# Graph attention on gathered rows: a third result buffer, 25 row buffers for 26, and another assignment of buffers and places to the row gathers

## The chip, the core and the metric

One core of one Trainium2 chip. The core has five engines with a queue each: TensorE (PE, with its weight loads shown as PEld), VectorE (DVE), ScalarE (ACT), GpSimd (POOL) and SyncE (SP). Each engine executes its own instructions strictly in the order in which they stand in its queue, and an instruction waits on semaphores for what other engines or transfers must have finished. The metric is device time of one execution in microseconds (us). Eleven runs of the kernel before gave a median of 1240.71 us, from 1235.78 to 1246.11.

## What is computed

```python
def _L0_gnn_ref(x, adj, Wf, bf, Wg, bg, W, bW):
    f = x @ Wf + bf
    g = x @ Wg + bg
    e = jax.nn.relu(f @ g.T)
    scores = jnp.where(adj > 0, e, -9e15)
    attention = jax.nn.softmax(scores, axis=1)
    return attention @ (x @ W + bW)

h = jnp.maximum(_layernorm(x, axis=-1), 0.0)
x = x + _L0_gnn_ref(h, adj, Wf, bf, Wg, bg, W, bW)
```

There are 3327 nodes with 1024 features in fp32. The adjacency has ones on its diagonal, is symmetric, and has few neighbours in a row (one entry in 208 or so), so that scores are needed only between a node and its neighbours.

## The kernel before

**Part 1 (to about 245 us)** reads the adjacency, sorts each row's neighbours into a list, normalises x into `hd` in DRAM, forms the product matrix `A_sb` of Wf and Wg on TensorE, and sorts the nodes by their number of neighbours, so that tiles of 128 nodes have like numbers. The change doesn't touch this part.

**Part 2 (from about 245 us)** handles 26 tiles of 128 nodes, t = 0 to 25, in the order of the list `ORDER`. `CAPS` says how many neighbours a tile's nodes have at most: 37 in the largest tile, which is t = 2, down to 11. The steps of a tile are named by letters in the kernel's own plan, and this text uses the same names:

- `L` (POOL): an indirect DMA brings the tile's lists of neighbours (128 short rows) into SBUF. `M` (DVE, L1197) makes a mask from them. `C` and `F` do the like for the few lists longer than 24.
- `H` (POOL): an indirect DMA gathers the tile's own 128 rows of `hd` (512 KB) into a row buffer. `hT`, `q` (PE) and `hc`, `qc`, `fq` (ACT) turn and multiply them to the query q of the tile.
- `G(t,k)` (POOL, L635): an indirect DMA gathers, for each of the 128 nodes, the row of its k-th neighbour (512 KB) into a row buffer.
- `d(t,k)` (DVE, L1222): the dot product of such a row with q, which gives a score. It is the first reader of the row.
- `S`, `T` (DVE) and `E`, `A`, `Y` (ACT): softmax of the scores, in one or two chunks of k.
- `s(t,k)` (DVE, L1272) adds row k, times its weight, to the tile's sum; or else `w(t,k)` (ACT, L1256) scales it and `p(t,k)` (PE, L1260) adds it in PSUM while it transposes. `SHARE` fixes which k go which way. The last of these readers frees the row buffer.
- `yt`, `W` (PE), `yc`, `fo` (ACT): the sum is turned and multiplied by W. `rc(t,o)` (ACT, L1298) copies the two halves of the result into a result buffer.
- `X(t)` (POOL): an indirect DMA adds the tile's rows of x to the result buffer; `O(t)` (POOL, L1305) then scatters the buffer to the output. The buffer is free when O has landed.

**The row buffers** (`G`, ROWS of them, 512 KB each) hold H rows and G rows. **The result buffers** (`xp`) are two; tile t uses buffer t mod 2, so `rc(t)` waits until `O(t-2)` has landed.

**The order** of all steps on PE, DVE, ACT and POOL is computed when the kernel is built, by a planner in the kernel's text. `steps_of` lists 2544 steps on these engines and on the DMA, each with the engine, how long it holds the engine, how long until its result can be used, and what it depends on. A gather is entered as 1.31 us on POOL and 3.2 us on the DMA, a list as 1.31 and 2.2 us, an output scatter as 1.31 and 3.2 us. `forward` simulates the engines with these figures, `backward` gives every step a rank, `planned` repeats both 30 times with small random changes of the ranks (fixed seed) and keeps the plan that ends first. The result is a list of (due time, step, row buffer). The kernel then emits the steps in the order of the due times. On the chip a due time is not a timer: what is left of the plan is the order on each engine and which buffer a row gets. A gather is issued when POOL reaches it and the last reader of its buffer has finished. In the plan before, a row takes the buffer that has been free for longest.

Of the kernel before, what the change touches and what calls it, by code (L numbers as in the profile page):

```python
# [13 lines left out]
ALU = mybir.AluOpType  # L14
# [22 lines left out]
QS = 2  # L37
WS = 2
TURNS = 6.0
ROWS = 26  # L40
PASSES = 30
SEED = 1
WIDE = 0.6
# [285 lines left out]
def steps_of():  # L329

    steps = {}

    def add(engine, takes, lasts, name, *deps, **kw):
        steps[name] = Step(name, engine, takes, lasts, deps, **kw)

    chunks = [split(s) for s in ORDER]
    n = len(ORDER)
    add("DVE", 0.15, 0.2, ("fl", 0), at=265.0)
    for t, s in enumerate(ORDER):
        cap, ends = CAPS[s], chunks[t]  # L340
        add("POOL", 1.31, 1.31, ("L", t), ("M", t - 3), *(("G", t - 3, k) for k in range(CAPS[ORDER[t - 3]] if t > 2 else 0)))
        add("DMA", 0.4, 2.2, ("Ld", t), ("L", t))
        if t > 1:
            add("POOL", 1.31, 1.31, ("H", t), row=True)
            add("DMA", 1.33, 3.2, ("Hd", t), ("H", t))
            for g in range(2):
                add("PE", 0.44, 0.66, ("hT", t, g), ("Hd", t), ("hc", t - 1, g), ("hT", t, g - 1), frees=[("H", t)] * g)
            for g in range(2):
                add("ACT", 0.49, 0.6, ("hc", t, g), ("hT", t, g), *(("q", t - 1, i, j) for i in range(3) for j in range(QS)))
            for i in range(3):  # L350
                for j in range(QS):
                    add(
                        "PE", 4.66 / QS, 4.66 / QS + 0.2, ("q", t, i, j), ("hc", t, 0), ("hc", t, 1), ("fq", 3 * t + i),
                        ("q", t, i, j - 1),
                    )
                add(
                    "ACT", 0.4, 0.52, ("qc", t, i), ("q", t, i, QS - 1),
                    *(("d", t - 2, k) for k in range(CAPS[ORDER[t - 2]])),
                )
                if 3 * t + i + 2 < 3 * n:  # L360
                    add("ACT", 0.38, 0.48, ("fq", 3 * t + i + 2), ("qc", t, i))
        used = [(op, t - 3, k) for op in "swY" for k in range(KM)]
        add("DVE", 0.16, 0.25, ("M", t), ("Ld", t), ("S", t - 3, 0), ("S", t - 3, 1), ("rc", t - 3, 0), ("rc", t - 3, 1), *used)
        if s < MORE:
            add("POOL", 1.31, 1.31, ("C", t), ("F", t - 1))
            add("DMA", 0.4, 2.5, ("Cd", t), ("C", t))
            add("DVE", 1.3, 1.4, ("F", t), ("Cd", t), *(("G", t - 1, k) for k in range(KL, CAPS[ORDER[t - 1]])))
        if t == n - 1:
            add("POOL", 1.31, 1.31, ("x", t), row=True)
            add("DMA", 1.33, 3.2, ("xd", t), ("x", t))  # L370
        summed = []
        for c, (k0, k1) in enumerate(ends):
            last = c == len(ends) - 1
            for k in range(k0, k1):
                late = [("F", t)] if k >= KL else [("hc", 2, 1) if k < 6 else ("qc", 2, 1)] if t == 1 else []
                add("POOL", 1.31, 1.31, ("G", t, k), ("Ld", t), *late, row=True)
                add("DMA", 1.33, 3.2, ("Gd", t, k), ("G", t, k))
                add(
                    "DVE", 1.2, 1.38, ("d", t, k), ("Gd", t, k), *(("qc", t, i) for i in range(3)),
                    ("M", t), at=(256.0, 266.0)[t] if t < 2 else 0.0,  # L380
                )
            add("DVE", 0.48 if c else 0.29, 0.6 if c else 0.41, ("S", t, c), *(("d", t, k) for k in range(k0, k1)), ("M", t))
            if c:
                add("ACT", 0.28, 0.33, ("A", t), ("S", t, c))
            add("ACT", 0.48, 0.55, ("E", t, c), ("S", t, c), ("fl", t))
            if c:
                add("ACT", 1.05, 1.15, ("Y", t, c), ("A", t), *(("s", t, k) for k in range(1, k0)))
            else:
                add("ACT", 1.05, 1.15, ("Y", t, c), ("E", t, c))
            add("DVE", 0.25 * c + 0.11 * last + 0.01, 0.25 + 0.2 * c, ("T", t, c), ("E", t, c), *([("A", t)] if c else []))  # L390
            for k in range(max(k0, 1), k1):
                if k in on_tensor(t):
                    add("ACT", 1.05, 1.15, ("w", t, k), ("E", t, c))
                    add("PE", 0.873, 1.07, ("p", t, k), ("w", t, k), ("yc", t - 1, 0), ("yc", t - 1, 1), frees=[("G", t, k)])
                    summed.append(("p", t, k))
                else:
                    add("DVE", 1.2, 1.28, ("s", t, k), ("E", t, c), ("Y", t, c), frees=[("G", t, k)])
                    summed.append(("s", t, k))
        for o in range(2):
            add("ACT", 0.62, 0.72, ("fo", t, o), ("rc", t - 1, o), ("T", t, len(ends) - 1))  # L400
        for g in range(2):
            add(
                "PE", 0.44, 0.66, ("yt", t, g), *summed, ("Y", t, len(ends) - 1), ("yc", t - 1, 0), ("yc", t - 1, 1),
                ("yt", t, g - 1),
                frees=[("G", t, 0)] * g,
            )
        for g in range(2):
            add("ACT", 0.49, 0.6, ("yc", t, g), ("yt", t, g), *(("W", t - 1, o, j) for o in range(2) for j in range(WS)))
        for o in range(2):
            for j in range(WS):  # L410
                add(
                    "PE", 7.0 / WS, 7.0 / WS + 0.2, ("W", t, o, j), ("yc", t, 0), ("yc", t, 1), ("fo", t, o),
                    ("W", t, o, j - 1),
                )
            if t < n - 1:
                add("ACT", 0.62, 0.72, ("rc", t, o), ("W", t, o, WS - 1), ("Od", t - 2))
            else:
                add("DVE", 0.6, 0.7, ("rc", t, o), ("W", t, o, WS - 1), ("Od", t - 2), ("xd", t), ("rc", t, o - 1), frees=[("x", t)] * o)
        if t < n - 1:
            add("POOL", 2.05, 2.05, ("X", t), ("rc", t, 0), ("rc", t, 1))  # L420
            add("DMA", 2.0, 4.5, ("Xd", t), ("X", t))
        add("POOL", 1.31, 1.31, ("O", t), ("Xd", t), ("rc", t, 0), ("rc", t, 1))
        add("DMA", 1.33, 3.2, ("Od", t), ("O", t))
    for step in steps.values():
        step.deps = [steps[d] for d in step.deps if d in steps]
        for d in step.deps:
            d.after.append(step)
    return list(steps.values())
# [121 lines left out]
def planned(rows, passes, seed=0, wide=1.0):  # L550
# [11 lines left out]
    for _ in range(passes):  # L562
# [7 lines left out]
        for k in steps:  # L570
            k.rank += chance.gauss(0, wide)
    return best


@with_exitstack
def edge_path(ctx: ExitStack, tc: tile.TileContext, x, adj, Wf, bf, Wg, bg, W, bW, out, flag):
# [57 lines left out]
    def gather(to, table, idx, **kw):  # L634
        return nc.gpsimd.indirect_dma_start(  # L635
            out=to,
            out_offset=None,
            in_=table,
            in_offset=bass.IndirectOffsetOnAxis(ap=idx, axis=0),
            **kw,  # L640
        )
# [484 lines left out]
    def tiles(name, n, shape, dtype=FP, **kw):  # L1126
        pool = ctx.enter_context(tc.tile_pool(name=name, bufs=n, reuse_waits="tile", **kw))
        return [pool.tile(shape, dtype, name=name) for _ in range(n)]

    with tc.manual_schedule(engines={  # L1130
# [6 lines left out]
        more = tiles("more", 1, [P, KM - KL], I32)[0]  # L1137
        hT = tiles("hT", 1, [P, KD, P])[0]
        yT = tiles("yT", 1, [P, KD, P])[0]
        res = tiles("xp", 2, [P, O])  # L1140
        junk = tiles("junk", 1, [P, D], BF)[0]
        scs = tiles("sc", 3, [P, KM])
        masks = tiles("mask", 3, [P, KM])
        nms, ls = tiles("nm", 6, [P, 1]), tiles("l", 6, [P, 1])
        als, rss = tiles("al", 3, [P, 1]), tiles("rs", 3, [P, 1])
        one, worst, onesf = tiles("one", 3, [P, 1])
        ps_q = tiles("p_q", 2, [P, CB], space=PSUM)
        ps_t = tiles("p_t", 2, [P, 4, P], space=PSUM)
        ps_y = tiles("p_y", 2, [P, 4, P], space=PSUM)
# [140 lines left out]
                )  # L1290

        def rc(t, o):
            to = res[t % 2][:, o * CB : (o + 1) * CB]
            if t == NT - 1:
                xr = G[buf["x", t]][:, o * CB : (o + 1) * CB]
                nc.vector.scalar_tensor_tensor(to, ps_o[o], rss[t % 3], xr, op0=ALU.mult, op1=ALU.add)  # L1296
            else:
                nc.scalar.activation(to, ps_o[o], AF.Copy, scale=rss[t % 3])  # L1298

        def X(t):  # L1300
            gather(res[t % 2], x[:, :], perm[:, ORDER[t] : ORDER[t] + 1], compute_op=ALU.add)

        def scatter(t):
            whole = ORDER[t] < N // P
# [2 lines left out]
                out_offset=bass.IndirectOffsetOnAxis(  # L1307
                    ap=perm[:, ORDER[t] : ORDER[t] + 1] if whole else final, axis=0
                ),
                in_=res[t % 2],  # L1310
                in_offset=None,
                bounds_check=None if whole else N - 1,
                oob_is_err=whole,
# [9 lines left out]
            "fq": fq, "d": dot, "S": greatest, "A": A, "E": E, "Y": Y, "T": T, "w": w, "p": p, "s": s, "fo": fo, "yt": yt,  # L1323
            "yc": yc, "W": project, "rc": rc, "X": X, "O": scatter,
        }
        plan = sorted(planned(ROWS, PASSES, SEED, WIDE)[1], key=lambda step: step[0])
        for start, (op, *at), held in plan:
            if held is not None:
                buf[(op, *at)] = held
            made[op](*at)  # L1330
# [41 lines left out]
```

## Time and profile before

| what | us |
|---|---|
| median of 11 runs | 1240.71 |
| the profiled execution | 1238.72 |
| its span (first to last instruction) | 1236.9 |
| DVE busy | 1131.5 |
| PE busy | 1111.9 |
| POOL busy | 874.0 |
| ACT busy | 617.3 |
| part 1, up to the last preparation on DVE | 243.3 |
| 454 G gathers: POOL time of one | 1.15 |
| 468 d: DVE time of one | 1.285 |
| 257 s: DVE time of one | 1.286 |

The mean granted clock of TensorE was 0.958 of full speed. DMA queue q0 carries what POOL issues and moved 290.96 MB of 374.46 MB. Busy shares say how full an engine is; what the end is made of shows where an engine that is full has to wait.

### The profile page before, as it was taken

What the parts mean: (1) busy time and instruction counts of PE and PEld (TensorE: products, weight loads), DVE (VectorE), ACT (ScalarE), POOL (GpSimd) and SP (SyncE); (2) the same over time, 40 slices, a digit from 0 to 9 for tenths busy, and PEclk for the clock granted to TensorE, in tenths of its full rate; (3) what the DMA queues carried; (4) which work ended last, traced back from release to release, by engine and by line L of the source; (5) the groups of instructions that cost most, each with busy time, mean ns of one, the idle gap of its engine ahead of it and who ended that gap; (6) DMA issues with size and microseconds to landing.
All of it is one profiled execution on the core that took longest, in us unless ns stands there. A gap on an engine that the chain in (4) does not pass through costs nothing. (4 is left out here: it accounts for less than half of the span.)

```text
span 1236.9 us, 14478 instructions
## 1 busy us (share of the span) xinstructions
PE 1111.9 (90%) x4632; PEld 711.1 (57%) x4632; DVE 1131.5 (91%) x2167; ACT 617.3 (50%) x941; POOL 874.0 (71%) x677
## 2 busy tenths in 40 slices
PE   2799981698889899998999999999998999999995
PEld 1566650466647466666765666665655665655552
DVE  5899987867999999999999999999999999999990
ACT  6899979225617266435644355444433333333260
POOL 8999986177577776777776777557667776777721
PEclk8799996799889999999999999999999999999998
DMA  9999996679858998989998998879988998899841
GB/s 367 418 402 404 410 350 249 243 275 370 301 208 291 350 304 318 332 315 306 337 331 286 321 323 313 274 216 349 322 291 263 324 279 300 273 321 300 297 123 53
DMA packets 101803, 374.46 MB, mean 303 GB/s; under 512 B 14747, under 2 KB 18490, under 8 KB 98519
## 3 DMA queue, kind: packets, MB, share of 16 engines
q0 software_dynamic: 80624, 290.96, 68.9%
q1 hardware_dynamic: 21094, 82.49, 17.3%
q8 instruction: 38, 0.62, 0.2%
q14 instruction: 47, 0.39, 0.1%
HBM read 344.11 MB, written 29.30 MB: 302 GB/s over the span
## 5 line engine op out<-in xcount | busy, mean ns | idle before, releaser
L635 POOL DMA_INDIRECT G<-hd,ps x454 | 521.6, 1149 | 212.3 <-issue 82.9
L1222 DVE CUSTOM_DVE_ANT_0 junk<-G,q 128x1024 bf16<-128x1024 f32 x468 | 601.3, 1285 | 27.5 <-DMA G<-hd,ps 19.5
L1287 PE MATMUL p_o<-W_sb,yT 128*128 128x512 f32 x832 | 366.2, 595 | 0.7 <-ACT yT L1283 0.7
L1209 PE MATMUL p_q<-A_sb,hT 128*128 128x342 f32 x1152 | 353.4, 456 | 6.8 <-ACT p_q L1218 6.1
L1272 DVE SCALAR_TENSOR_TENSOR G<-G,sc 128x1024 f32<-128x1024 f32 x257 | 330.4, 1286 | 3.0 <-ACT G L1245 1.9
L1209 PEld LDWEIGHTS p_q<-A_sb,hT 128*128 128x128 f32 x1152 | 213.8, 191 | 112.0 <-issue 9.7
L1287 PEld LDWEIGHTS p_o<-W_sb,yT 128*128 128x128 f32 x832 | 157.1, 190 | 189.8 <-issue 183.1
L1260 PE MATMUL p_y<-ident,G 128*128 128x128 f32 x1688 | 206.5, 276 | 25.4 <-ACT G L1256 18.5
L1260 PEld LDWEIGHTS p_y<-ident,G 128*128 128x128 f32 x1688 | 190.4, 142 | 57.6 <-ACT G L1256 27.8
L1256 ACT ACTIVATE G<-G,sc 128x1024 f32<-128x1024 f32 x185 | 197.2, 1137 | 0.1
L698 POOL TENSOR_TENSOR r<-r,iotaj 128x1664 f32<-128x1664 f32 (+3 forms) x50 | 183.7, 3712 | 11.2 <-ACT r L691 11.2
L831 PE MATMUL ps_A<-WgT,WfT 128*128 128x342 f32 x432 | 132.4, 466 | 2.2 <-ACT WfT L826 2.2
L1298 ACT ACTIVATE xp<-p_o,rs 128x512 f32<-128x512 f32 x50 | 33.1, 681 | 195.0 <-DMA out_dram<-xp,perm 123.2
L761 DVE MAX8 cand<-r 128x8 f32<-128x208 f32 (+2 forms) x416 | 119.0, 360 | 4.3 <-POOL r L698 3.4
L831 PEld LDWEIGHTS ps_A<-WgT,WfT 128*128 128x128 f32 x432 | 82.6, 195 | 43.5 <-issue 3.7
L1215 ACT COPY q<-p_q 128x342 f32<-128x342 f32 x72 | 31.6, 443 | 103.2 <-DVE sc L1222 65.9
L691 ACT ACTIVATE r<-r 128x3327 f32<-128x3327 int32 (+3 forms) x27 | 77.3, 2863 | 8.6 <-DMA r<-in_adj_dram 8.6
L1241 ACT ACTIVATE sc<-sc,nm 128x10 f32<-128x10 f32 (+10 forms) x36 | 11.0, 305 | 121.7 <-DVE nm L1231 104.9
L1283 ACT COPY yT<-p_y 128x512 f32<-128x512 f32 x52 | 30.0, 585 | 51.9 <-PE p_y L1260 51.9
L635 POOL DMA_INDIRECT xp<-in_x_dram,perm x25 | 40.3, 1611 | 19.9 <-ACT xp L1298 12.9
L1305 POOL DMA_INDIRECT out_dram<-xp,perm x25 | 30.1, 1204 | 30.4 <-DMA xp<-in_x_dram,perm 24.9
L1205 ACT COPY hT<-p_t 128x512 f32<-128x512 f32 x48 | 27.2, 587 | 45.0 <-PE p_q L1209 24.5
(139 smaller groups left out, 703.3 us busy)
## 6 DMA issues: line engine op xcount, KB each, us to landing
r<-in_adj_dram SPq DMA_DIRECT2D x24, 1663.5 KB, 11.4
xt<-in_x_dram SPq DMA_DIRECT2D x25, 512.0 KB, 12.3
hd<-xt SPq DMA_DIRECT2D x25, 512.0 KB, 10.5
G<-hd,ps POOLq DMA_INDIRECT x454, 6.3
A_sb<-in_L_gnn_Wg_dram SPq DMA_DIRECT2D x8, 512.0 KB, 17.4
A_sb<-in_L_gnn_Wf_dram SPq DMA_DIRECT2D x8, 512.0 KB, 10.7
W_sb<-in_L_gnn_W_dram POOLq DMA_DIRECT2D x1, 4096.0 KB, 18.0
cd<-cand SPq DMA_DIRECT2D x25, 64.0 KB, 11.4
```

What stands on the lines that cost most here:

```text
L635: return nc.gpsimd.indirect_dma_start(out=to, out_offset=None, in_=table, in_offset=bass.IndirectOffsetOnAxis(ap=idx, axis=0), **kw,)
L691: nc.scalar.activation(r[:n, b:e], a[:n, b:e], AF.Sign, accum_out=to)
L698: eng.tensor_mul(r[:n, b:e], r[:n, b:e], iotaj[:n, b:e])
L761: nc.vector.max(cands[t][:n, s * 8 : s * 8 + 8], r[:n, s * SW : min(N, (s + 1) * SW)])
L831: nc.tensor.matmul(ps[:, :QB], WfTs[c][:, k, :], WgT[:, k, o : o + QB], start=(k == 0), stop=(k == KD - 1))
L1209: nc.tensor.matmul(ps_q[(3 * t + i) % 2][:, :QB], hT[:, k, :], A_sb[:, k, i * QB : (i + 1) * QB], start=False, stop=(k == KD - 1), skip_gr ...
L1222: nc.vector.tensor_tensor_reduce(junk, row(t, k), q[:, :D], 1.0, q[:, D : D + 1], op0=ALU.mult, op1=ALU.add, accum_out=scs[t % 3][:, k : k ...
L1256: nc.scalar.activation(g, g, AF.Copy, scale=scs[t % 3][:, k : k + 1])
L1260: nc.tensor.matmul(ps_y[g][:, c, :], of[:, (4 * g + c) * P : (4 * g + c + 1) * P], ident, is_transpose=True, start=((t, g) not in begun an ...
L1272: nc.vector.scalar_tensor_tensor(y, row(t, k), scs[t % 3][:, k : k + 1], y, op0=ALU.mult, op1=ALU.add)
L1287: nc.tensor.matmul(ps_o[o], yT[:, k, :], W_sb[:, k, o * CB : (o + 1) * CB], start=False, stop=(k == KD - 1), skip_group_check=True,)
L1298: nc.scalar.activation(to, ps_o[o], AF.Copy, scale=rss[t % 3])
```

## The change

It has four parts. A third result buffer: tile t uses buffer t mod 3, and `rc(t)` waits for `O(t-3)`. One row buffer less (25), which gives back the SBUF that this takes. The gathers G of the tile t = 1 no longer wait in the plan for steps of the query of t = 2. And a function `paced` goes over the finished plan: it keeps the order of every engine, but moves the due times of POOL's steps and gives the rows other buffers. A row is due at the earliest 1.7 us after the row before it (`SPACE`), unless its first reader is due within 9 us (`LEAD`), and it takes the buffer that came free last before its due time, in place of the one that has been free for longest. The new plan is a new result of the planner, since the number of buffers and two sorts of dependency are other, and so the order of steps differs on all engines. Between two output scatters that follow each other on POOL a one-column memset is put (this occurs twice).

```diff
-ROWS = 26
+ROWS = 25
+RESULTS = 3
+LEAD = 9.0
+SPACE = 1.7
...
-                late = [("F", t)] if k >= KL else [("hc", 2, 1) if k < 6 else ("qc", 2, 1)] if t == 1 else []
-                add("POOL", 1.31, 1.31, ("G", t, k), ("Ld", t), *late, row=True)
+                add("POOL", 1.31, 1.31, ("G", t, k), ("Ld", t), *([("F", t)] if k >= KL else []), row=True)
...
-                add("ACT", 0.62, 0.72, ("rc", t, o), ("W", t, o, WS - 1), ("Od", t - 2))
+                add("ACT", 0.62, 0.72, ("rc", t, o), ("W", t, o, WS - 1), ("Od", t - RESULTS))
...
+def paced(plan, rows):
+
+    steps = {k.name: k for k in steps_of()}
+    start = {name: begun for begun, name, _ in plan}
+    end = {}
+    for k in steps.values():
+        for name in k.frees:
+            end[name] = start[k.name] + k.lasts + 2 * HOP
+    pool = []
+    for begun, name, held in plan:
+        if steps[name].engine == "POOL":
+            last = begun
+            if steps[name].row:
+                last = min(start[a.name] for d in steps[name].after if d.engine == "DMA" for a in d.after) - LEAD
+            pool.append((begun, name, last))
+    now, before, free = 0.0, 0.0, [(0.0, i) for i in range(rows)]
+    for begun, name, last in sorted(pool):
+        step = steps[name]
+        if step.row:
+            now = max(now, begun, min(before + SPACE, last), min(free)[0])
+            at, i = max((at, i) for at, i in free if at <= now)
+            free.remove((at, i))
+            free.append((end[name], i))
+            step.buf, before = i, now
+        start[name] = now = max(now, begun)
+        now += step.takes
+    return sorted(((start[name], name, steps[name].buf) for _, name, _ in plan), key=lambda step: step[0])
...
-        res = tiles("xp", 2, [P, O])
+        res = tiles("xp", RESULTS, [P, O])
...
-            to = res[t % 2][:, o * CB : (o + 1) * CB]
+            to = res[t % RESULTS][:, o * CB : (o + 1) * CB]
...
-        plan = sorted(planned(ROWS, PASSES, SEED, WIDE)[1], key=lambda step: step[0])
+        plan = paced(planned(ROWS, PASSES, SEED, WIDE)[1], ROWS)
+        issued = None
         for start, (op, *at), held in plan:
+            if op in ("L", "H", "x", "C", "G", "X", "O"):
+                if op == issued == "O":
+                    nc.gpsimd.memset(between, 0.0)
+                issued = op
```

More of the change, by code (lines that the diff above doesn't have):

```diff
@@ L415, in steps_of @@
             if t < n - 1:
-                add("ACT", 0.62, 0.72, ("rc", t, o), ("W", t, o, WS - 1), ("Od", t - 2))
+                add("ACT", 0.62, 0.72, ("rc", t, o), ("W", t, o, WS - 1), ("Od", t - RESULTS))
             else:
-                add("DVE", 0.6, 0.7, ("rc", t, o), ("W", t, o, WS - 1), ("Od", t - 2), ("xd", t), ("rc", t, o - 1), frees=[("x", t)] * o)
+                add("DVE", 0.6, 0.7, ("rc", t, o), ("W", t, o, WS - 1), ("Od", t - RESULTS), ("xd", t), ("rc", t, o - 1), frees=[("x", t)] * o)
         if t < n - 1:
@@ L1145, in edge_path @@
         als, rss = tiles("al", 3, [P, 1]), tiles("rs", 3, [P, 1])
-        one, worst, onesf = tiles("one", 3, [P, 1])
+        one, worst, onesf, between = tiles("one", 4, [P, 1])
         ps_q = tiles("p_q", 2, [P, CB], space=PSUM)
@@ L1300, in X @@
         def X(t):
-            gather(res[t % 2], x[:, :], perm[:, ORDER[t] : ORDER[t] + 1], compute_op=ALU.add)
+            gather(res[t % RESULTS], x[:, :], perm[:, ORDER[t] : ORDER[t] + 1], compute_op=ALU.add)
         def scatter(t):
@@ L1309, in scatter @@
                 ),
-                in_=res[t % 2],
+                in_=res[t % RESULTS],
                 in_offset=None,
```

## The prediction, made before the changed kernel had run

> **What bounds the kernel now.** I read the page first, then busy time by stretches, then who waits for whom, then single waits in the order of time.
>
> ```profile
> PE 1111.9 (90%) x4632; PEld 711.1 (57%) x4632; DVE 1131.5 (91%) x2167; ACT 617.3 (50%) x941; POOL 874.0 (71%) x677
> 500.00:740.00 240.00, 233.13 (x1036) 151.12 (x1035) 236.76 (x360) 118.06 (x182) 177.03 (x153) 1.00 0.92 318
> 740.00:980.00 240.00, 232.44 (x965) 146.53 (x964) 234.88 (x331) 100.61 (x157) 163.42 (x140) 0.99 0.86 294
> ```
>
> In the stretches the columns are PE, PEld, DVE, ACT and POOL busy. From 500 us on DVE is busy 236.8 and 234.9 of 240 us, PE 233.1 and 232.4 (modelled ends, so less than it looks). DVE's work can't be shortened by an order, so what this change can win or lose is DVE's idle time. Between 262 and 1200 us that is little:
>
> ```profile
> DVE junk L1222 <- DMA G<-hd,ps: 14.4, 17, 3.9
> DVE mask L1197 <- DMA ps<-pd,perm: 2.9, 2, 1.8
> DVE G L1272 <- ACT G L1245: 1.9, 2, 1.0
> DVE rs L1252 <- ACT sc L1241: 0.9, 2, 0.5
> ```
>
> Total, times, longest: 20.1 us in all, 17.3 of them waits for a gather (d for its row, M for its list). That is the whole stake here, 1.6% of 1236.9.
>
> **A law for these waits.** I ran the kernel's planner (plain Python) for both versions and matched its steps with the trace. I take no time from it, only distances: by how much a reader is due after its transfer is due on POOL. Call lateness the start in the trace less the due time. DVE must wait when lateness of POOL + landing time − distance exceeds DVE's own lateness. The list of t = 6 shows it: POOL issued it 13.4 us late, M is due 3.9 us after it, and it landed after 4.8 us; 13.4 + 4.8 − 3.9 = 14.3, and M started 14.3 us late, from 12.5 before:
>
> ```profile
> 489.88 1.03 POOL L635 DMA_INDIRECT ps<-pd,perm  x1 [0.30 <-issue]
> ...
> 494.68 0.29 DVE L1197 TENSOR_SCALAR mask<-iotak,ps 128x40 f32<-128x40 f32 x1 [1.77 <-DMA ps<-pd,perm]
> ```
>
> It holds for M(15) (15.4 + 5.7 − 4.5 = 16.6, found 16.6) and d(3,6) (8.1 + 6.7 − 5.7 = 9.1, found 9.3). DVE's lateness grows from 0 to 21.3 us by 1188 us and never comes down, for DVE is hardly idle by plan except at both ends. POOL's lateness is DVE's plus 0 to 1 us, since its gathers wait for rows that DVE frees. So a wait costs about **landing − distance**, and every one is paid at the end.
>
> Landing times, issue to landing (median us), over 500 to 900 us, and in the sparse stretch 340 to 362 us:
>
> ```profile
> G<-hd,ps POOLq DMA_INDIRECT x203, 6.3
> ...
> ps<-pd,perm POOLq DMA_INDIRECT x11, 5.3
> ```
>
> ```profile
> G<-hd,more POOLq DMA_INDIRECT x8, 5.4
> ```
>
> **The change part by part.** Instructions are the same in number and shape (468 d, 257 s, 493 gathered H, G and x rows) but for two one-column memsets; DVE's nearest row, a one-column memset, took 0.06 us, and POOL waits there for the last result anyway: 0 us. The reordering of PE, DVE and ACT takes no work away: 0, and its waits are in the terms below. Of 493 rows, the distance to the reader is under 6.3 us for 50 before and 87 after, and under 4.55 us for none before and 18 after; the median falls from 13.9 to 9.8 us. `paced` does this: it delays rows whose own reader is far, and what stands behind them on POOL, lists and scatters too, moves back without being asked. Net terms, after minus before, on DVE:
>
> 1. *Start to 331 us.* The first d now stands behind L(1), H(2), L(0) and two G of t = 1: G(0,0) can issue at about 253.2 (251.4 before) and its d start near 259.1 (255.78 before). Against that, two rows are in hand when it does, so the waits of 2.33 and 0.80 us at 259 and 261 us go. Later H(3) and G(2,0..2) are only 2.9 to 3.3 us ahead of their readers (6.3 − 3.0 = 3.3 us of wait, as long as the 3.9 us of before at 291.8), and G(2,12) 3.8 us. Walking the list with pitch 1.28 us and landing 6.2 us I get DVE 7.2 us late at S(2,0), against 6.7 in the trace: **+0.5** (−4 if the late rows cost nothing more, +5 if PE's wait for H(3) is paid again).
>
> 2. *Second chunk of t = 2, some 333 to 365 us.* All buffers are full there; each G waits for an s to free a row:
>
> ```profile
> 341.93 1.74 POOL L635 DMA_INDIRECT G<-hd,more  x1 [3.48 <-DVE G L1272]
> 344.32 1.75 POOL L635 DMA_INDIRECT G<-hd,more  x1 [0.66 <-DVE G L1272]
> 346.73 1.75 POOL L635 DMA_INDIRECT G<-hd,more  x1 [0.66 <-DVE G L1272]
> ...
> 340.38 1.28 DVE L1272 SCALAR_TENSOR_TENSOR G<-G,sc 128x1024 f32<-128x1024 f32 x1
> ```
>
> Before, the rows had 9.4 us and DVE never waited here. After, one buffer less and an H more in hand leave 4.6 us for twelve rows in turn. The s of 340.38 ends at 341.66, the gather goes at 341.93: 1.28 + 0.27 + 5.4 = 6.95 us from the start of s to the landing, where the plan has 1.42 + 4.6 = 6.0. Excess 0.95 us. A first wait shifts the next two s alike, so it recurs at every third row: 4 × 0.95 = **+3.8** (0.8 with the shortest landings here, about 4.6; 7.4 with 6.3).
>
> 3. *Lists that come late.* Distance from L to M falls for t = 5 from 18.2 to 2.6 us, t = 6 from 3.9 to 2.6, t = 8 from 30 to 3.3, t = 10 from 12.7 to 2.5, and rises for t = 15 from 4.5 to 16.2. At 4.9 us landing: t = 5 **+2.3**; t = 6 2.3 where 1.8 was paid, **+0.5**; t = 8 1.6, halved because PE, less late than DVE, frees the rows ahead of it, **+0.8**; t = 10 2.4, less for the same reason, **+1.5**; t = 15 −1.1, which rows of t = 14 and 15 with 5.0 us (5.6 before) take back with 6.3 − 5.0 = 1.3: **0**. Low end of them all −1 (lists of before also landed in 2.3 us), high end +9.
>
> 4. *Third result buffer.* ACT stands 123 us at rc for scatters, but nearly always with nothing behind it that is wanted. The longest of these waits did reach DVE, for 0.93 us (PE waited 0.91 us for ACT at the same place):
>
> ```profile
> 952.49 1.27 ACT L1298 ACTIVATE xp<-p_o,rs 128x512 f32<-128x512 f32 x2 [11.68 <-DMA out_dram<-xp,perm]
> ...
> 958.17 1.29 DVE L1272 SCALAR_TENSOR_TENSOR G<-G,sc 128x1024 f32<-128x1024 f32 x1 [0.93 <-ACT G L1245]
> ```
>
> The new plan spends the room: O is due under 6 us ahead of the rc that needs its buffer in 11 tiles (6 before), twice only 2.3 us. Behind a waiting rc stand ACT's E and w, and for those wait DVE's s and PE's p. **0** (−2 to +3).
>
> 5. *Wider spacing.* By the two landing rows above, 6.3 us in the dense stream and 5.4 at one gather per 2.4 us, 1.7 us of pitch should give some 0.2 us each on the waits that stay: **−1** (0 to −6, the last if all landings came down to 5.4).
>
> Sum: 0.5 + 3.8 + 2.3 + 0.5 + 0.8 + 1.5 + 0 + 0 − 1 = **+8.4 us**. On the profiled 1238.72 that is 1247.1; the median lies 2.0 above that execution, so **1249.1**, 0.68% slower.
>
> *A rule against the row.* The trace shows 5.4 to 6.3 us from issue to landing for a 512 KB gather. The Trainium skill, "DMA: Bandwidth & Descriptors", section on the anatomy of one DMA, gives about 2.0 us and the bytes at 436 GB/s, 3.2 us, which is the figure the planner has too. By that rule a distance of 4.6 us is enough: term 2 vanishes, the lists (3.1 us with POOL's 1 us) cost 0.5 or 0.6 where they come 2.5 ahead, and the sum is about +1. The rows decide, since M(6) and d(3,6) waited just as they say.
>
> **Rivals.**
>
> *A wash.* The rows land in 4.2 to 4.9 us where the pitch is 2.4 us, as the quickest here did, and lists in 2.3 to 3.3 us: terms 1 to 3 give 0.5 + 0.8 + 0.5, the buffer −0.9, spacing −1: −0.1, so about **1240.6**. For it: spacing takes load off the queue. Against it: 5.4 is the median at a pitch already wider than 1.7.
>
> *Faster.* The spacing is what the queue lacks: fewer rows ahead of each list, scatter and H. If landings fall to 5.4, about 0.9 of each of the 17 gather waits of before goes. Term 5 at its end (−6), lists at −1, term 2 at 0.8, term 1 at 0.5: −5.7, **1235.0**. It decides if G's median landing is below 5.5 us between 500 and 900 us. Against it: landing hardly moved between the dense stretch of 280 to 310 us (median 6.5) and the rest (6.3).
>
> *Much slower: a row tied to its last reader.* With the buffer freed last, the gather issues only some 0.9 us (median) after its release by plan, 2.2 before. If PE or ACT are late once (PE waited 4.7 us for ACT's w at 313 us), POOL stands, and all rows behind it come late; one such block, about 2 us, in each of 10 further tiles: 1249 + 11 to 20 = **1260 to 1269**. It decides if POOL's lateness runs over 2 us above DVE's.
>
> *That it doesn't do what it says*: due times are no timers, and the first 25 buffers are free, so nothing is spaced before some 285 us. That is already in term 1.
>
> **How the numbers follow.** Forecast 1249, own range 1244 to 1256: 0.50. Much slower: 0.10. Wash: 0.13. Faster: 0.27. A change under 0.2% (2.5 us) can't be told from none with these runs. So faster 0.27, same 0.13, slower 0.60. The range for 8 in 10 leaves out most of the much slower case and the lower part of the faster one: 1234 to 1258.
>
> **What would show it.** Right: DVE's idle before L1222 and L1197 released by a DMA, between 262 and 1200 us, near 25 us (17.3 now); waits of about 1 us at every third d between 335 and 370 us; M waiting about 2 us near 460, 500 and 660 us. G's median landing at 500 to 900 us 6.0 to 6.3 us. Wrong: that idle time below 15 us, lists landing within 3 us, or landing at 5.5. The prediction falls altogether if DVE's idle time falls and the end still moves back, for then PE sets the end.

## The result, and the profile after

The changed kernel takes 1271.26 us (median of 8 runs, 1267.64 to 1275.86), the kernel before 1241.35 beside it (31 runs): a ratio of 1.0243, 95% interval 1.0226 to 1.026. It is 30 us slower; 8.4 us slower was forecast, with 1258 as the upper end of the range. The sign was right, the size was not.

In three of the five sets of runs below the kernel before itself took 1268 to 1287 us on the chip, for a reason that I couldn't find; those sets are told, but nothing is concluded from them, and the numbers of the other experiments are from the two sets in which it took 1240 us.

From the page after: the span, the total busy time of the engines, and the group of ACT's copies into the result buffers with its idle time before them; below them, the same group from the page before.

```profile
span 1271.7 us, 14375 instructions
...
PE 1121.0 (88%) x4632; PEld 721.2 (57%) x4632; DVE 1130.8 (89%) x2167; ACT 618.8 (49%) x941; POOL 891.4 (70%) x679
...
L1329 ACT ACTIVATE xp<-p_o,rs 128x512 f32<-128x512 f32 x50 | 33.3, 683 | 232.9 <-DMA out_dram<-xp,perm 145.4
```

```profile
L1298 ACT ACTIVATE xp<-p_o,rs 128x512 f32<-128x512 f32 x50 | 33.1, 681 | 195.0 <-DMA out_dram<-xp,perm 123.2
```

DVE is busy for 1130.8 us (1131.5 before): its work is unchanged, so the 34.8 us of longer span are idle time of DVE, as the prediction had it. With a third result buffer ACT waits longer for scatters (145.4 us) than with two (123.2).

Where the idle time is, by stretches of the execution (length; PE, PEld, DVE, ACT, POOL busy; granted clock, DMA share, GB/s), three lines from after and then the middle stretch from before:

```profile
0.00:240.00 240.00, 168.23 (x666) 112.79 (x667) 205.78 (x795) 189.83 (x280) 198.36 (x105) 0.89 0.94 358
240.00:262.00 22.00, 22.00 (x83) 14.68 (x82) 5.74 (x21) 4.09 (x9) 10.44 (x11) 1.00 0.66 224
262.00:1200.00 938.00, 874.36 (x3678) 563.00 (x3676) 879.46 (x1297) 401.17 (x619) 660.39 (x546) 0.97 0.87 292
```

```profile
262.00:1200.00 938.00, 897.33 (x3799) 570.56 (x3798) 907.66 (x1335) 416.15 (x643) 660.90 (x558) 0.99 0.88 301
```

DVE was busy 206.59, 8.28 and 907.66 us in the same stretches before. So it lost 0.8 us in part 1 (which the change doesn't touch), 2.5 at the start of part 2, 907.66 − 879.46 = 28.2 between 262 and 1200 us, and the remaining 3.9 us of idle time at the end, 1.35 of them in the last wait for `p_o` (14.14, from 12.79): 35.4 us together, as DVE's busy time is 0.7 us less. TensorE's granted clock was 0.97 in the middle stretch, from 0.99, but no wait of DVE there is put down to PE. Most of the idle time is in the middle, and there the waits of DVE after are (total, times, longest):

```profile
DVE junk L1253 <- DMA G<-hd,ps: 30.0, 31, 3.1
DVE mask L1228 <- DMA ps<-pd,perm: 9.2, 4, 4.0
DVE junk L1253 <- DMA G<-hd,more: 3.8, 5, 1.1
DVE G L1303 <- ACT G L1276: 1.8, 1, 1.8
DVE found L1218 <- DMA cts<-cd,perm: 1.3, 1, 1.3
DVE junk L1253 <- ACT hT L1236: 1.2, 1, 1.2
...
```

Waits for a transfer come to 30.0 + 9.2 + 3.8 + 1.3 = 44.3 us, from 17.3: 41 waits for 19, of hardly greater size (1.08 us each, 0.91 before). The readers wait at the kind of place that the prediction named, but at twice as many.

Landing is not what changed. Issues of POOL between 500 and 900 us after, with the median us to landing:

```profile
G<-hd,ps POOLq DMA_INDIRECT x196, 6.1
ps<-pd,perm POOLq DMA_INDIRECT x11, 5.2
```

They are 6.1 and 5.2 us, where before had 6.3 and 5.3. The spacing made the gathers hardly quicker; what fell is the distance from the due time of a gather to that of its reader.

Put against the plan, DVE's lateness (the start in the trace less the due time) grows like this; the forecast column adds the prediction's terms:

| stretch | grows before | grows after | net | forecast |
|---|---|---|---|---|
| start to S(2,0), 331 us | 6.7 | 10.1 | +3.4 | +0.5 |
| second chunk of t = 2, to 384 us | 0.9 | 4.4 | +3.5 | +3.8 |
| rows of t = 3, to the first wait for t = 4 | 3.1 | 5.9 | +2.8 | none |
| t = 4 to 7, to 545 us | 3.6 | 12.9 | +9.3 | +2.8 |
| to 800 us (lists of t = 8 and 10) | 1.1 | 8.1 | +7.0 | +2.3 |
| rows of t = 14 and 15, to 880 us | 1.2 | 7.2 | +6.0 | 0 |
| to the last s | 4.3 | 6.9 | +2.6 | 0 (spacing −1) |
| sum | 20.9 | 55.5 | +34.6 | +8.4 |

**A late list is paid for twice.** The worst place after is around the list of t = 5. The timeline has start, duration, engine, line, and in brackets the idle time before the instruction with its releaser.

```profile
469.00 0.97 POOL L666 DMA_INDIRECT ps<-pd,perm  x1 [0.30 <-issue]
...
474.31 0.24 DVE L1228 TENSOR_SCALAR mask<-iotak,ps 128x40 f32<-128x40 f32 x1 [3.96 <-DMA ps<-pd,perm]
...
482.47 1.28 DVE L1253 CUSTOM_DVE_ANT_0 junk<-G,q 128x1024 bf16<-128x1024 f32 x1 [1.38 <-DMA G<-hd,ps]
```

DVE came to M(5) 21.6 us late. POOL issued the list 22.8 us late, it landed 5.3 us later, and the plan has 2.6 us between them: 22.8 + 5.3 − 2.6 = 25.5, and M started 25.6 us late. The law of the prediction holds, here as at every other wait of a d or an M for a transfer over 0.3 us in this stretch, to 0.2 us. What follows is what the prediction left out. The gather for d(5,1) goes 25.4 us late: POOL has caught up with DVE's new lateness, since its gathers wait for rows that DVE frees. Its distance is 3.6 us and it lands in 5.1: 25.4 + 5.1 − 3.6 = 26.9, and d(5,1) starts 27.1 us late. The next gather that is waited for goes 28.0 us late, with 5.8 us of distance and 5.6 of landing, and costs 0.65 us. So a group of short distances costs not its worst member once: whenever POOL has caught up, the next short distance is charged again in full. In all, the shortfalls (what landing exceeds the distance by, with 6.2 us for rows and 4.9 for lists) add up to 116 us in the plan after and 38 before. One new wait of the middle has another cause, a scatter; it is told under term 4 below.

The same law at the place that the prediction had right, the second chunk of t = 2, where each gather waits for an s:

```profile
349.58 1.28 DVE L1253 CUSTOM_DVE_ANT_0 junk<-G,q 128x1024 bf16<-128x1024 f32 x1 [1.09 <-DMA G<-hd,more]
...
357.83 1.28 DVE L1253 CUSTOM_DVE_ANT_0 junk<-G,q 128x1024 bf16<-128x1024 f32 x1 [0.96 <-DMA G<-hd,more]
...
365.69 1.28 DVE L1253 CUSTOM_DVE_ANT_0 junk<-G,q 128x1024 bf16<-128x1024 f32 x1 [0.56 <-DMA G<-hd,more]
...
373.85 1.28 DVE L1253 CUSTOM_DVE_ANT_0 junk<-G,q 128x1024 bf16<-128x1024 f32 x1 [0.78 <-DMA G<-hd,more]
```

One wait at every third or fourth row, 3.4 us in these four, as worked out: here the recurrence was counted.

### The profile page after: what moved, and what is told of

Same layout as the page of the kernel before. It is cut to its first block, busy times and chain, and to the rows that moved or that the text cites. A ratio compares the mean times of both kernels' runs of the same rounds, so it can differ in the third digit from the quotient of the medians.

```text
span 1271.7 us, 14375 instructions
## 1 busy us (share of the span) xinstructions
PE 1121.0 (88%) x4632; PEld 721.2 (57%) x4632; DVE 1130.8 (89%) x2167; ACT 618.8 (49%) x941; POOL 891.4 (70%) x679
## 5 line engine op out<-in xcount | busy, mean ns | idle before, releaser
L666 POOL DMA_INDIRECT G<-hd,ps x454 | 542.3, 1195 | 226.0 <-issue 91.3
L1291 PE MATMUL p_y<-ident,G 128*128 128x128 f32 x1688 | 212.1, 281 | 32.7 <-ACT G L1287 25.4
L1291 PEld LDWEIGHTS p_y<-ident,G 128*128 128x128 f32 x1688 | 196.7, 145 | 60.9 <-ACT G L1287 32.8
L729 POOL TENSOR_TENSOR r<-r,iotaj 128x1664 f32<-128x1664 f32 (+3 forms) x50 | 183.8, 3705 | 12.2 <-ACT r L722 12.2
L1329 ACT ACTIVATE xp<-p_o,rs 128x512 f32<-128x512 f32 x50 | 33.3, 683 | 232.9 <-DMA out_dram<-xp,perm 145.4
L846 PE MATMUL ps_tr<-ident,A_sb 128*128 128x128 f32 x128 | 23.1, 345 | 26.5 <-DMA A_sb<-in_L_gnn_Wg_dram 23.3
L666 POOL DMA_INDIRECT ps<-pd,perm x26 | 27.5, 1056 | 25.6 <-DMA cd<-cand 18.0
## 6 DMA issues: line engine op xcount, KB each, us to landing
xt<-in_x_dram SPq DMA_DIRECT2D x25, 512.0 KB, 12.4
A_sb<-in_L_gnn_Wg_dram SPq DMA_DIRECT2D x8, 512.0 KB, 17.2
```

Of the source, the lines that this page charges most:

```text
L666: return nc.gpsimd.indirect_dma_start(out=to, out_offset=None, in_=table, in_offset=bass.IndirectOffsetOnAxis(ap=idx, axis=0), **kw,)
L729: eng.tensor_mul(r[:n, b:e], r[:n, b:e], iotaj[:n, b:e])
L1291: nc.tensor.matmul(ps_y[g][:, c, :], of[:, (4 * g + c) * P : (4 * g + c + 1) * P], ident, is_transpose=True, start=((t, g) not in begun an ...
```

## The experiments

Theory A is that of the prediction: the cost is made of short distances between gathers and their readers, charged by the law above. Its rivals are named in each expectation; in short, B puts the cost on the new plan whatever its distances, C on the tie of a row to the buffer that was freed last, and D on any new draw of the plan.

All runs in the sets in which the kernel before took 1240 us (ratio to it with 95% interval). "Waits" are DVE's waits for transfers between 275 and 1200 us, which leaves out the very first rows, and "first d" is when the first dot product started.

| kernel | us | ratio | waits | first d |
|---|---|---|---|---|
| before | 1240.16 and 1240.77 | 1 | 15.3 | 255.8 |
| after | 1271.26 | 1.0243 (1.0226 to 1.026) | 43.3 | 260.2 |
| after, not paced | 1260.28 | 1.017 (1.0142 to 1.0197) | 27.5 | 259.9 |
| before, paced | 1252.6 | 1.0096 (1.0069 to 1.0124) | 24.9 | 256.8 |
| after, newest buffer, no space | 1264.09 | 1.0173 (1.0133 to 1.0214) | 34.7 | 260.5 |
| before, t = 1 free | 1252.19 | 1.01 (1.0072 to 1.0128) | 18.8 | 260.6 |
| after, true landings | 1250.82 | 1.009 (1.0056 to 1.0124) | 18.1 | 259.6 |
| before, true landings | 1240.43 | 0.9992 (0.9977 to 1.0007) | 12.4 | 265.0 |
| after, not paced, two result buffers | 1259.88 | 1.0152 (1.0116 to 1.0189) | 30.6 | 260.3 |

**1. The changed kernel without `paced`.** The new plan with its oldest free buffers.

```diff
-plan = paced(planned(ROWS, PASSES, SEED, WIDE)[1], ROWS)
+plan = sorted(planned(ROWS, PASSES, SEED, WIDE)[1], key=lambda step: step[0])
```

> The changed kernel without paced: 25 row buffers, three result buffers, no extra wait for tile 1, the plan as the planner leaves it. Every engine has the same order as in the changed kernel; only the row buffers differ (136 of 493 rows keep their predecessor). Theory A (a gather whose row or list is due on POOL too near its reader makes VectorE wait; the shortfalls against landing, 6.2 us for a row and 4.9 us for a list, sum to 38 us before, 116 us in the changed kernel, 65 us here; 30 us of time for 78 us of shortfall, 0.39 each): 1251 us, VectorE waiting some 25 to 30 us for gathers and lists between 262 us and the end of the dot products. Theory B (the new order of the steps, from 25 buffers and three result buffers, costs it all): 1271 us, as the changed kernel. Theory B' (paced costs it all): 1241 us.

1260.28 us, between A and B: `paced` makes 11 of the 30 us and the new plan about 20. A had it the other way round, 11 for the new plan and 20 for `paced`.

**2. `paced` on the plan before.** 26 rows, two result buffers, the wait of t = 1 kept.

```diff
-plan = sorted(planned(ROWS, PASSES, SEED, WIDE)[1], key=lambda step: step[0])
+plan = paced(planned(ROWS, PASSES, SEED, WIDE)[1], ROWS)
```

> The kernel before with paced alone: 26 row buffers, two result buffers, the old extra wait for tile 1, the old order of steps on every engine, other buffers for the rows. Theory A: shortfalls of 71 us, 1254 us. Theory B: 1241 us. Theory B': 1271 us. If the two parts add up, this and the kernel without paced together bring 30 us over before.

1252.6 us, as A had it (1254). The waits rise by 9.6 us of the 12.4. So the two halves roughly add: 12 for `paced` on the old plan and 20 for the new plan come near the 30 of both.

**3. The tie to the newest buffer, without the spacing.**

```diff
-SPACE = 1.7
+SPACE = 1.31
```

> The changed kernel with SPACE 1.31 us, which is what a gather takes on POOL: paced moves almost no due time, but each row still takes the buffer that came free last. Shortfalls sum to 68 us. Theory A: 1252 us, the same as without paced. Theory C (what costs is that a gather is tied to the release just before it, so that any lateness of the releaser passes to POOL and to all rows behind, whatever the spacing): 1262 to 1271 us, with POOL later than VectorE by over 2 us.

1264.09 us. That is in the range that C gave, but the range was reckoned from 1251 or so for the kernel without `paced`, which took 1260.28: by the medians the tie itself costs 4 us (the two intervals overlap, and one of the four runs took 1256.55, so it may be nothing), and the other 7 of `paced` come with the spacing. The sign that C named, POOL over 2 us later than DVE, shows at one wait of this trace, that of M(8) with 2.4 us, and at no other wait of 0.5 us or more for a row or a list. The spacing can act only through the buffers: due times are no timers, and `paced` with the oldest free buffer leaves the order of every engine and the buffer of every row as they were. A later due time only makes another buffer the one that was freed last, and on the chip the gather then waits for the last reader of that one, nearer to its own reader.

**4. Only the wait of t = 1 taken out of the plan before.** 26 rows, two result buffers, not paced.

```diff
-late = [("F", t)] if k >= KL else [("hc", 2, 1) if k < 6 else ("qc", 2, 1)] if t == 1 else []
+late = [("F", t)] if k >= KL else []
```

> The kernel before with one edit: the gathers of tile 1 no longer wait in the plan for the query of tile 2 (26 row buffers, two result buffers, no paced). Shortfalls sum to 33 us against 38; the plan's own end is 2.5 us later. Theory A: 1241 us, within 2.5 us of before. Theory B, if this edit is the part of the new order that costs: 1255 us or more.

1252.19 us, a miss for A, which had 1241, and short of the 1255 that B asked for. The waits rise by only 3.5 us. The rest is at the two ends: the first d starts at 260.6 us (255.8 before, with part 1 ending 2.2 us later in this execution, so 2.6 us of it are the order), since L(1), H(2) and rows of t = 1 now go ahead; and the last tile's `p_o` keeps DVE waiting 15.59 us, from 12.79. The sum of the shortfalls is 33 here, less than before, so it doesn't give the size of a new plan by itself: two rows landed in 8.1 and 8.2 us and cost 2.8 and 2.7 us.

**5. The whole change, with a planner that knows the landing times of the trace.** If A is right, the cost should go although nothing of the change is undone. Rows get 4.9 us (behind 1.31 on POOL), lists 3.6, scatters 4.7, the gather of x into the result buffer 6.0.

```diff
-add("DMA", 0.4, 2.2, ("Ld", t), ("L", t))
+add("DMA", 0.4, 3.6, ("Ld", t), ("L", t))
...
-add("DMA", 1.33, 3.2, ("Gd", t, k), ("G", t, k))
+add("DMA", 1.33, 4.9, ("Gd", t, k), ("G", t, k))
...
-add("DMA", 1.33, 3.2, ("Od", t), ("O", t))
+add("DMA", 1.33, 4.7, ("Od", t), ("O", t))
```

> The changed kernel with all its parts and true landings in the planner (row 4.9, list 3.6, add 6.0, scatter 4.7 us after POOL's part), for a time at which the kernel before takes 1240 us; in two earlier calls it took 1286 and 1287, and this kernel 1263 and 1266. Theory A (distances shorter than landings cost the 30 us of the change): 1242 to 1250 us, VectorE's waits for gathers and lists between 262 us and its last dot product 10 to 23 us, against 46 in the changed kernel. Theory B (25 buffers, three result buffers or paced as such): 1263 us or more, as in the two calls before.

1250.82 us, just above the 1242 to 1250 of A: 20 of the 30 us come back, with the third buffer, 25 rows and `paced` all in place. DVE's waits between 275 and 1200 us in this run:

```profile
DVE junk L1253 <- DMA G<-hd,ps: 13.5, 20, 2.2
DVE mask L1228 <- DMA ps<-pd,perm: 4.1, 2, 2.7
DVE rs L1283 <- ACT sc L1272: 1.8, 3, 0.9
DVE G L1303 <- ACT G L1276: 1.0, 1, 1.0
DVE junk L1253 <- DMA G<-hd,more: 0.5, 1, 0.5
...
```

18.1 us for transfers, where the same change with 3.2 us in the planner has 43.3. That is the strongest evidence for A: 25 of the 28 us of new waits went with the short distances (the two profiled executions took 1273.43 and 1247.34 us). It is a new draw of the plan too, so the times alone would not show it; the waits do.

**6. The same figures for the kernel before** (with seed 39, the one of 40 whose plan ends first; run 5 kept seed 1).

> The kernel before with true landings in the planner and seed 39, for a time at which the kernel before takes 1240 us (at 1286 us of it, this one took 1298). Theory A: 1233 to 1239 us. Theory D (the plan of before happens to fit the chip): 1245 to 1255 us.

1240.43 us, no gain: a miss for A and for D, which had 1245 or more. The waits fall by 2.9 us, but the plan's own end moves back by 6.9 us, and the first d starts at 265.0 us (part 1 ended 3.7 us later than in the profile of before). The 12.4 us of waits that remain are in a plan with no shortfall: a late landing (8.1 us for one row) or a POOL up to 1.8 us later than DVE is enough, so short distances explain what the change added and not every wait. With true landings on both sides the change costs 10 us, with 3.2 us on both sides 30; but 7 of these 10 are already the difference between the two plans' own ends, 13.7 us later in run 5 and 6.9 here, and only one of the two had its seed chosen.

**7. One result buffer less, not paced.**

```diff
-RESULTS = 3
+RESULTS = 2
```

> The kernel without paced with two result buffers in place of three, for a time at which the kernel before takes 1240 us: 1258 to 1263 us if the third result buffer is worth next to nothing (1260 with three), 1270 if its worth is 10 us.

1259.88 us, against 1260.28 with three: the third result buffer is worth nothing that can be measured here, though the two are also two draws of the plan. The planner fills the room that it gives with another order: by the prediction's count, in 11 tiles of the plan after a scatter is due under 6 us before its buffer is needed, from 6.

**8. Runs that settle nothing.** The kernel before took 1286.96 us in the second set, 1285.82 in the third and 1267.83 in the fifth. In the traces of these sets ACT, PE and DVE stand idle with no releaser in sight. Three waits of ACT between 275 and 1200 us, from the fifth set's run of the kernel before with another seed:

```profile
ACT hT L1205 <- remote: 43.2, 9, 17.0
...
ACT q L1215 <- issue: 25.9, 6, 10.7
...
ACT xp L1298 <- issue: 20.5, 2, 12.0
```

"remote" and "issue" mean that no instruction or transfer in the profile released it. That is first of all a gap in the record: these traces hold no landing time for any transfer that POOL issued, where the traces of the other sets do. Many of these waits stand at steps where the same kernel waits in the other sets too, for an engine that has a name there: the copy of `yT` that waited 12.7 us without one at 940 us, in the third set's run of the whole change with true landings, waited 9.5 us for PE at 926 us in the run of experiment 5. And they recur: in all three runs with the other seed the same copy of `hT` waits 17.0 to 17.2 us. So what took the time in these sets isn't known, and what their traces put a wait down to carries little weight.

The whole change with true landings, twice:

> The changed kernel with all its parts, but the planner is told how long transfers take on the chip: after 1.31 us on POOL a row 4.9 us (3.2 in the plan so far), a list 3.6 (2.2), the add of x 6.0 (4.5), a scatter 4.7 (3.2). Shortfalls sum to 8 us in place of 116; the plan's own end is 13.7 us later. Theory A (distances shorter than landings cost the 30 us): VectorE's lateness against the plan falls from 56 us to 10 or 15, so 1242 to 1247 us; waits of VectorE for gathers and lists under 15 us. Theory B (what costs is 25 buffers, three result buffers or paced as such, whatever the planner knows of landings): 1270 us or more, waits as in the changed kernel (over 40 us).

1262.91 us, a ratio of 0.9823 (0.9747 to 0.99), and again 1265.65, 0.9832 (0.977 to 0.9894): faster than the kernel before there, while it is slower than it where that takes 1240. Without `paced`, twice:

> The kernel without paced (25 row buffers, three result buffers) with the same true landings in the planner: no shortfall left. Theory A: 1240 to 1245 us, against 1260 without true landings; paced costs here 0 to 4 us, since it finds few rows to bring too near. Theory B: 1260 us.

> For a time when the kernel before takes 1240 us. The changed kernel without paced, and the planner told of the landing times of the trace (rows 4.9 us behind 1.31 on POOL, lists 3.6, output scatters 4.7). Theory A (paced costs what it takes away from the distances, whatever the plan): it lies below the same kernel with paced, which took 1250.8, by 4 to 10 us: 1241 to 1247. Rival B (with true landings in the plan paced has nothing left to spoil): 1249 to 1253. Rival C (the new orders with 25 buffers are simply poor, and true landings helped by another accident of the order): 1255 to 1265.

1295.7 us, and 1282.33 with a ratio of 1.0123 (0.9994 to 1.0252). So whether `paced` still costs where distances are true stays open.

The kernel before with another seed and nothing else, three times:

> The kernel before with another seed of the planner (4 for 1) and nothing else. The plan's own end is 4.0 us later, shortfalls are 53 us against 38. Theory A as a sum (0.39 for each us of shortfall): 1240 + 4 + 6 = 1250 us. Theory D (the plan of before happens to fit the chip, and any new plan made with short landings loses some 10 to 15 us beyond its own end, whatever the edit): 1254 to 1260 us.

> For a time when the kernel before takes 1240 us. The kernel before with another random seed of its planner and nothing else. It asks how much of the 20 us that stay without paced is only that a plan was drawn again. Theory D (a new draw by a planner that believes in 3.2 us landings costs 10 to 20 us by itself): 1250 to 1260. Theory A (the rules that were changed cost, not the draw): 1237 to 1245.

1290.34 us (0.9961), 1287.48 (1.002), and 1285.8 with 1.0149 (1.0012 to 1.0286). D is neither shown nor refuted by these times. Two result buffers without `paced` gave 1287.2 (0.9987) and 1281.69 (1.0085) in these sets, and the kernel before with true landings 1297.63 (1.0137).

Last, a version that was to beat both: 26 rows, two result buffers, not paced, t = 1 free, true landings, seed 14 and smaller random changes.

> For a time when the kernel before takes 1240 us. 26 row buffers and two result buffers as before, no paced, only the dependency of the tile t = 1 is gone, and the planner is told of true landing times (other seed, smaller random changes; its plan ends earliest of those tried). If the stalls for rows and lists are what an order can win: DVE's waits for them fall under 10 us and the time is 1230 to 1237. If they only move to PE and ACT: 1238 to 1245.

1290.52 us, 1.0175 (1.0047 to 1.0303), in the fifth set. DVE's waits for transfers were put at 11.0 us between 275 and 1200 us, and 57 us went on waits for ACT, which itself waited with no releaser in sight, so what it would take where the kernel before takes 1240 us isn't known. No version that beats the kernel before was found.

## Why the prediction was right in its law and wrong in its sum

**What bounds the kernel: right.** DVE's work didn't change, and 28.2 of the 35.4 us of new idle time lie in the middle stretch, 27.0 of them as waits for transfers. The law "lateness of POOL plus landing less distance" gave each of these waits.

**Term 1, the start: mis-sized.** +0.5 was forecast, +3.4 measured. The place was right (rows and H of t = 2 some 3 to 5 us ahead of their readers), and the walk down the list found too few: after the first rows, F(2) and d(2,1), d(2,5), d(2,7) and d(2,12) waited 1.25, 1.21, 1.06, 0.56 and 1.90 us (the trace puts the second down to ACT, though the law fits it). In the five kernels with t = 1 free and 3.2 us in the planner the first d started at 259.9 to 260.6 us, near the 259.1 of the forecast.

**Term 2, the second chunk of t = 2: right.** +3.8 forecast, +3.5 measured, at every third or fourth row.

**Term 3, lists and rows: the step that failed.** It charged each late list once and set "rows 14/15" and the rows near the lists to nothing, and it had no term for the rows of t = 3 at all. Forecast 5.1 us; measured +9.3, +7.0 and +6.0 where it had 2.8, 2.3 and 0, and +2.8 for t = 3: 25.1 in all. Of the 8.1 us after behind that +7.0, 4.3 are the waits of M(8) and M(10) and 1.75 are a wait for ACT (term 4). Two things make the rest of that gap. A late list itself cost more than its own landing less distance, when POOL was later than DVE to begin with: M(5) 3.96 us for 2.3 (POOL 1.2 us later than DVE), M(8) 3.26 for 0.8 (1.6 us later), where the halving "because PE, less late than DVE, frees the rows" was a guess that the trace didn't follow; M(10) 1.01 for 1.5 and M(6) 0.94 for 2.3 went the other way, as POOL was earlier than DVE there. And POOL catches up with DVE after each wait, so the short rows behind a late list were charged as well: the prediction had counted this in term 2, where one buffer recurs, and not elsewhere. For t = 14 and 15, "rows of 5.0 us, 5.6 before" were netted against the list of t = 15; four rows there waited in turn:

```profile
839.21 1.28 DVE L1253 CUSTOM_DVE_ANT_0 junk<-G,q 128x1024 bf16<-128x1024 f32 x1 [2.04 <-DMA G<-hd,ps]
...
860.95 1.29 DVE L1253 CUSTOM_DVE_ANT_0 junk<-G,q 128x1024 bf16<-128x1024 f32 x1 [2.73 <-DMA G<-hd,ps]
...
871.20 1.28 DVE L1253 CUSTOM_DVE_ANT_0 junk<-G,q 128x1024 bf16<-128x1024 f32 x1 [1.12 <-DMA G<-hd,ps]
...
873.16 1.28 DVE L1253 CUSTOM_DVE_ANT_0 junk<-G,q 128x1024 bf16<-128x1024 f32 x1 [0.67 <-DMA G<-hd,ps]
```

That is 6.6 us. The row of 860.95 had landed after 8.3 us, the others after 5.3 to 6.2.

**Term 4, the third buffer: right** at about 0, as the pair 1260.28 and 1259.88 bears out. The reason was right too: ACT's wait for scatters grew, and little came of it. Little isn't nothing: a copy into a result buffer waited 17.28 us, ACT then worked through what stood behind it without a pause, and the first sum that needed ACT's scaling of row 0 made DVE wait.

```profile
617.26 0.69 ACT L1329 ACTIVATE xp<-p_o,rs 128x512 f32<-128x512 f32 x1 [17.28 <-DMA out_dram<-xp,perm]
...
629.42 1.28 DVE L1303 SCALAR_TENSOR_TENSOR G<-G,sc 128x1024 f32<-128x1024 f32 x1 [1.75 <-ACT G L1276]
```

That is 1.75 us for the 0.93 of before, inside the term's −2 to +3. The prediction called the 11.68 us at 952 us the longest of ACT's waits for a scatter; the longest before was 16.38 us, at 428 us, and no wait of DVE for ACT or PE followed it.

**Term 5, the spacing: wrong sign as a part of the sum.** −1 was forecast from quicker landings. They fell by 0.2 us, as forecast, but what the spacing takes from the distances belongs in the same term, and `paced` alone cost 12 us (on the new plan 11, some 7 of them with the spacing). The prediction had listed the loss of distance (87 rows under 6.3 us for 50, 18 under 4.55 for none) and didn't turn that count into a price.

**The rivals.** A wash and the faster case fell: G's median landing stayed above 5.5 us. (The wash took landings of 4.2 to 4.9 us at a pitch of 2.4 us as seen; the quickest of the nine gathers there landed in 4.9 us and the next in 5.2.) "Much slower" came nearest in size (1260 to 1269) and not by its mechanism: it decides if POOL's lateness runs over 2 us above DVE's, and at the waits of 0.5 us and more it was at most 1.7 us above, more often below. The signs named beforehand: landing of 6.0 to 6.3 us was right (6.1), DVE's waits of 25 us were wrong (44.3), M waiting near 460, 500 and 660 us was right in kind (474, 520 and 686 us) and uneven in size (3.96, 0.94 and 1.01 us), and M(8) at 596 us waited 3.26.

**The rule against the row.** The Trainium skill, "DMA: Bandwidth & Descriptors", section on the anatomy of one DMA, gives about 2.0 us and the bytes at 436 GB/s, which is an estimate of 3.2 us for the 512 KB of a gather. The median here is 6.1 to 6.3 us from issue to landing, about 5 of it behind the 1.15 to 1.20 us on POOL, and the lists, 128 short rows, took 5.2 to 5.3. The measurement decides. The planner holds the same 3.2 us behind its 1.31 on POOL, and with the traced figures in its place 20 of the 30 us came back.

**What stays open.** Why the new plan has more short distances, and costs about 20 us without `paced`: in its profile (an execution of 1257.23 us) 12.2 us more are waits for transfers between 275 and 1200 us, and DVE is idle 1.9 us more from 240 to 262 us and 3.3 us more behind 1200 us (1.35 of these in the last wait for `p_o`); a plan is drawn anew with other rules, and these can't be told from the draw. D, any new draw, is thus neither shown nor excluded for these 20 us. Whether another draw by the same rules would cost as much could not be told in the sets where the kernel before took 1268 to 1287 us; in the trace of the last of them the other seed's waits for transfers are put at 18.4 us, near the 15.3 of the kernel before, but that trace has no landing times, so this settles nothing. With 25 rows and the old wait of t = 1 the planner finds no plan at all, so these two parts could not be tried apart on the chip.

## What to carry to other kernels

Where the order is fixed when the kernel is built, look at how far each transfer is issued ahead of its reader, and compare that with the landing time in the trace: spreading issues out takes that distance away, and here the quicker landing (0.2 us) didn't pay for it. Add up every short distance behind which the issuing engine can catch up, not the worst of a group. And before rearranging a plan, put the measured landing times into it: that took 20 us off the changed kernel here, though it gained nothing for the kernel before.

## What the hardware showed that I had not expected

A small list (128 short rows) takes nearly as long as a 512 KB gather when it stands behind gathers: 5.2 us for 6.1, against 3.3 us for the list of t = 0 at the start of part 2 in the run after. In each of the traces with landing times the slowest gather took 8.1 to 9.2 us; three of 8.1 to 8.3 us whose distance was under 6.5 us cost 2.7 to 2.8 us each.

Part 1, the same in all kernels, ended between 243.25 and 246.99 us in the profiled executions, so a difference of 2 or 3 us between the starts of part 2 in two single profiles can be that alone.
